# A gated MLP with quantised activations: a row of scales read back a slot later, POOL's scaling of weights moved ahead of its sums, two start loads exchanged, and the warm-up matmuls dealt out anew

## The chip, the cores and the metric

The kernel runs on one core of one Trainium2 chip. Such a core has a matrix engine (PE, TensorE) and three engines for elementwise work: DVE (VectorE), ACT (ScalarE) and POOL (GpSimd). SP (SyncE) computes nothing and issues transfers (DMAs). Each engine takes its instructions strictly in the order in which they are written for it. The metric is the time of one execution in microseconds on the device.

## The reference

There are 4 sequences of 1024 tokens with 512 features (`x`), a condition row of 128 numbers for each sequence (`cond`), and three weights: `norm_w` (512 x 128), `up_w` (4096 x 512) and `down_w` (512 x 2048).

```python
scale = cond @ norm_w.T + 1.0                    # one row of 512 scales for each sequence
ms = mean(x * x, axis=-1)
h = x * (scale[:, None, :] * rsqrt(ms + 1e-6))
u = h @ up_w.T
val, gate = split(u, 2, axis=-1)
h = val * gelu(gate)
hq = act_quant(h)        # rows scaled to +-127 by their largest value, rounded, scaled back
wq = weight_quant(down_w)                        # -1, 0 or 1 times mean(abs(down_w))
y = hq @ wq.T + x
```

## The kernel before

**Batches and slots.** The work goes batch by batch (`b`, a sequence of 1024 tokens, in two halves of 512) and in each batch slot by slot (`j`, 0 to 15, each 128 of the 2048 hidden features, with their gate and value rows of `up_w`). In the first batch the up product is made plainly: `plain_half(j, h)` makes the gate (12 matmuls, `pg`), its GELU on ACT, the value (12 matmuls, `pv`), and their product on DVE (L513). While it does so, it also prepares the weights for the later batches, which use a scheme with 7 products instead of 8 (`slot`, `product`). The lines that the change touches all lie in the first batch and its start.

**The weights of a slot** go through these steps: `w_load(j)` (SP, L244) fetches two tiles of 128x512; `w_range(j)` (DVE, L249 to L254) finds a power of two for every row and its inverse `iv`; `w_gain(j)` (DVE, L257); `w_scale(j)` multiplies the tiles by `iv` (L265, on POOL unless said otherwise); `w_turn(j)` transposes them on PE (L273) into two PSUM banks `pw`; `w_high(j)` (ACT, L286 to L289), `w_evac(j)` (ACT, L302) and `w_low(j)` (DVE, L295 to L298) take them out as a high and a low f16 part and as f32. From the f32 copy POOL makes four sums (`s_sums`, L306 to L309), ACT their high parts (`s_high`, L317), POOL their low parts (`s_low`, L321); SP writes the slot's 896 KB to DRAM (`s_spill`, L324). `s_all(j)` is s_high, s_low and s_spill. The tile that a spill has read is filled again three slots later, by `w_high`.

PSUM banks rotate: tag A has two, B one, E two, `po` three. A matmul or transpose that writes a bank waits until everything that reads the bank's earlier content is done. `pw`, `pm` and `pd` share the three banks of `po` from slot 1 on.

**The scales of cond.** `cond_scale(0)` (DVE, L160) makes batch 0's row at the start from `nw` (norm_w) and `cb` (cond's row read to all 128 partitions), both loaded on ACT's queue. `cond_largest`, `cond_over` (a PE transpose, `pm`), `cond_range`, `cond_spread` (a PE matmul, `pd`) and `cond_undo` make from it a power of two for the batch. The rows of batches 1 to 3 are made on DVE later (`cond_scale_rest`), written to DRAM four bytes at a time by `cond_rows` (SP, L214) in slot 3, and read back by `cond_load_scale(b)` (SP, L219) as a tile that all partitions hold. `cond_bring` (DVE, L223) multiplies the tile by the batch's power of two. The row of batch 1 is used first by `Tokens.scale` in slot 6.

**The start.** DVE makes an identity matrix and zeros (`warm`), from which `keep_warm(n)` issues n matmuls of 128x512 that nobody reads. The tokens of the first half are loaded in pairs (`first_load`), summed (`first_sum`, ACT, L712), scaled by the inverse root (`rsqrt_start`, ACT and DVE; `first_scale`, L729 on ACT or L731 on DVE), transposed (`first_turn`, PE, L736, four transposes for each of the tiles 0 to 3 into four banks `ptx`), and taken out by `first_high` (ACT, L740) and `first_low` (DVE, L744). The first matmuls of slot 0 (L527) follow the first_high steps one by one.

**Order.** In the start and the first batch the order is the order of the calls, written out by hand under a manual schedule; there is no planner there. Each call appends its instructions to the queues of its engines. The stretch that matters stands at lines 924 to 982, and this piece of it in slot 4 is the reading back:

```python
for j in range(3, NJ):
    if j == 4:
        sc = cond_load_scale(1)
        cond_bring(1, sc)
    first_batch(j, sc if j >= 4 else None)
```

Of the kernel before, what the change touches and what calls it, by code (L numbers as in the profile page):

```python
# [41 lines left out]
def glu_quant_kernel(  # L42
# [10 lines left out]
    PE, ACT, DVE, POOL, SP = nc.tensor, nc.scalar, nc.vector, nc.gpsimd, nc.sync  # L53
# [79 lines left out]
    def pow2_floor(t):  # L133

        ti = t.bitcast(I32)
        DVE.tensor_scalar(ti, ti, EXPONENT, None, ALU.bitwise_and)

    def bank(tag, bufs, shape=None, name=None):
        return psum.tile(shape or [P, TOK], F32, name=name or tag, tag=tag, bufs=bufs)

    def po_bank(name, shape=None):
        return bank("po", 3, shape, name)
# [10 lines left out]
    def cond_load(b0, b1):  # L153

        v = cond[b0:b1].rearrange("b c -> (b c)").partition_broadcast(P)
        ACT.dma_start(out=cb[:, b0:b1].rearrange("p b c -> p (b c)"), in_=v)
# [47 lines left out]
    def cond_undo(pd, b0, b1):  # L204
        DVE.tensor_copy(dx[:, b0:b1], pd)
        DVE.reciprocal(ux[:, b0:b1], dx[:, b0:b1])
# [9 lines left out]
    def cond_load_scale(b):  # L216

        sc = wpool.tile([P, D], F32, name=f"sc_{b}", tag="sc", bufs=1)
        SP.dma_start(out=sc, in_=rows_dram[b].partition_broadcast(P))  # L219
        return sc  # L220

    def cond_bring(b, sc):
        DVE.tensor_scalar(sc, sc, ux[:, b : b + 1], None, ALU.mult)  # L223
# [9 lines left out]
    def wn(j):  # L233
        return H[:, W_SLOT[j % 3]]

    def wf(j):

        return H[:, 11 if j == 2 else 15 + j % 2].rearrange("p t (n f) -> p (t n) f", n=2)
# [3 lines left out]
    def w_load(j, ts=(1, 0)):  # L242
        for t in ts:
            SP.dma_start(out=wn(j)[:, t], in_=up_v[j][:, t])  # L244

    def w_range(j, t0=0, t1=2):
        t = slice(t0, t1)
        am = sm.tile([P, 2], F32, name=f"wam_{j}_{t0}", tag="wam")[:, t]
        DVE.tensor_reduce(am, wn(j)[:, t], AX.X, ALU.max, apply_absolute_value=True)  # L249
        pow2_floor(am)  # L250
        DVE.tensor_scalar(sw[:, j, t], am, 2.0**-100, 1.0 / W_UP, ALU.max, ALU.mult)
        if j not in iv:
            iv[j] = sm.tile([P, 2], F32, name=f"iv_{j}", tag="iv", bufs=3)
        DVE.reciprocal(iv[j][:, t], sw[:, j, t])  # L254

    def w_gain(j):
        DVE.tensor_scalar(sg0[:, j, :], sw[:, j, :], dx[:, 0:1], None, ALU.mult)  # L257

    def w_scale(j, ts=(1, 0), eng=POOL):
        for t in ts:  # L260
            w, r = wn(j)[:, t], iv[j][:, t : t + 1]
            if eng is ACT:
                ACT.activation(w, w, AF.Copy, scale=r)
            else:
                eng.tensor_scalar(w, w, r, 1.0, ALU.mult, ALU.mult)  # L265

    def w_turn(j, banks=None, ts=(1, 0)):
        if j not in pw:
            pw[j] = banks or [po_bank(f"pw_{j}_{t}") for t in (1, 0)]
        for t in ts:  # L270
            n = 1 - t
            for k in range(NK):
                PE.transpose(  # L273
                    pw[j][n][:, k * P : (k + 1) * P], wn(j)[:, t, k * P : (k + 1) * P], ident
                )

    def a_parts(j):

        s = s_tile(j)
        return s[:, 0:2], A21[:, j % 3], s[:, 5]  # L280

    def w_high(j, ts=(1, 0)):
        gate, a21, a22 = a_parts(j)
        g, v = (p.rearrange("p (n f) -> p n f", n=2) for p in pw[j])
        if 1 in ts:
            ACT.copy(gate[:, :, 0], g)  # L286
        if 0 in ts:
            ACT.copy(a21[:, 0], v[:, 0])
            ACT.copy(a22[:, 0], v[:, 1])  # L289
# [14 lines left out]
    def s_sums(j):  # L304
        a11, a12, a21, a22 = (wf(j)[:, n] for n in range(4))
        POOL.tensor_tensor(sf[:, 0], a21, a22, ALU.add)  # L306
        POOL.tensor_tensor(sf[:, 2], a11, a21, ALU.subtract)
        POOL.tensor_tensor(sf[:, 1], sf[:, 0], a11, ALU.subtract)
        POOL.tensor_tensor(sf[:, 3], a12, sf[:, 1], ALU.subtract)  # L309
# [166 lines left out]
    def plain(j, t, h, ps):  # L476

        gate, a21, a22 = a_parts(j)
        a = [gate[:, 0], gate[:, 1]] if t else [a21, a22]
        a = [v.rearrange("p w (k f) -> p w k f", k=2) for v in a]  # L480
        terms = [(w, 1 - w, k) for k in range(NK) for w in (1, 0)]
        high = [(0, 0, k) for k in range(NK)]
        terms = high + terms if j < 2 else terms + high
        for n, (w, l, k) in enumerate(terms):
            PE.matmul(  # L485
                ps, a[k // 2][:, w, k % 2, :], XP[:, l, k, h * TOK : (h + 1) * TOK],
                start=n == 0, stop=n == len(terms) - 1,
            )
# [7 lines left out]
    def gain(g, t):  # L496
        return sg[g // NJ][:, g % NJ, t : t + 1]

    def h_half(g, h):
        return h_slots(g)[:, 0, h]  # L500
# [4 lines left out]
    def plain_half(j, h, between=nothing):  # L505
        pg = bank("A", 2, name=f"pg_{j}_{h}") if h else bank("B", 1, name=f"pg_{j}_{h}")
        plain(j, 1, h, pg)
        t1 = wpool.tile([P, TOK], F32, name=f"g_{j}_{h}", tag="t1")
        ACT.activation(t1, pg, AF.Gelu, scale=gain(j, 1))
        between()  # L510
        pv = bank("E", 2, name=f"pv_{j}_{h}")
        plain(j, 0, h, pv)
        DVE.scalar_tensor_tensor(h_half(j, h), pv, gain(j, 0), t1, ALU.mult, ALU.mult)  # L513
# [176 lines left out]
    start_t = sm.tile([P, 1], F32, name="start_t", bufs=1)  # L690
    eps = sm.tile([P, 1], F32, name="eps", bufs=1)
    DVE.memset(eps, EPS)
    ACT.dma_start(out=nw, in_=norm_w.rearrange("(k p) c -> p k c", p=P))
    cond_load(0, 1)
    ACT.activation(start_t, one, AF.Sqrt)


# [8 lines left out]
    ssq0 = sm.tile([P, 8], F32, name="ssq0", bufs=1)  # L706
    rs0 = sm.tile([P, 8], F32, name="rs0", bufs=1)
# [8 lines left out]
    def rsqrt_start(t, y):  # L716

        z = sm.tile([P, 2], F32, name="newton", tag="newton")
        ACT.activation(z, t, AF.Sqrt, scale=1.0 / D, bias=eps)
        DVE.tensor_scalar(t, t, 1.0 / D, EPS, ALU.mult, ALU.add)  # L720
        DVE.reciprocal(y, z)
        DVE.tensor_tensor(z, y, y, ALU.mult)
        DVE.scalar_tensor_tensor(z, z, -0.5, t, ALU.mult, ALU.mult)
        DVE.scalar_tensor_tensor(y, z, 1.5, y, ALU.add, ALU.mult)

    def first_scale(n, eng):
        r = rs0[:, n : n + 1]
        if eng is ACT:
            ACT.activation(X0[:, n], X0[:, n], AF.Copy, scale=r)  # L729
        else:  # L730
            eng.tensor_scalar(X0[:, n], X0[:, n], r, 1.0, ALU.mult, ALU.mult)  # L731

    def first_turn(n, pts):
        for k in range(NK):
            c = (n % NA) * P
            PE.transpose(pts[k][:, c : c + P], X0[:, n, k * P : (k + 1) * P], ident)  # L736
# [11 lines left out]
    def keep_warm(n):  # L748

        pz = bank("A", 2, name="pz")  # L750
        for i in range(n):
            PE.matmul(pz, warm[:, :P], warm, start=True, stop=True)
# [6 lines left out]
    first_load(4)  # L759
    first_load(6)  # L760
    w_load(2)
    keep_warm(12)
    first_sum(0)
    first_sum(1)
    cond_scale(0)
    mx = cond_largest(0, 1)
    pm = cond_over(mx, 0, 1, "A")
    rsqrt_start(ssq0[:, 0:2], rs0[:, 0:2])
    keep_warm(3)
    pd = cond_spread(cond_range(pm, 0, 1), 0, 1, "A")  # L770
    keep_warm(1)
    first_sum(2)
    first_scale(0, ACT)
    first_sum(3)
    w_range(0, 1, 2)
    first_scale(1, DVE)
    rsqrt_start(ssq0[:, 2:4], rs0[:, 2:4])
    w_scale(0, (1,), ACT)
    first_scale(2, ACT)
    cond_undo(pd, 0, 1)  # L780
    cond_bring_first()
    first_scale(3, DVE)
    ptx = [po_bank(f"ptx_0_{k}") for k in range(3)] + [bank("A", 2, name="ptx_0_3")]
    first_turn(0, ptx)
    keep_warm(2)
    first_turn(1, ptx)
    w_turn(0, [bank("E", 2, name=f"pw_0_{t}") for t in (1, 0)], (1,))
    first_turn(2, ptx)
    first_turn(3, ptx)
    w_high(0, (1,))  # L790
    w_range(0, 0, 1)
    w_scale(0, (0,), DVE)
    w_gain(0)
# [125 lines left out]
    def s_all(j):  # L919
        s_high(j)  # L920
        s_low(j, POOL)
        s_spill(j)
# [21 lines left out]
    cond_scale_rest()  # L944
    mx = cond_largest(1, B)
    plain_half(0, 1)
    s_all(1)
    s_sums(2)
    w_range(4)
    w_gain(4)  # L950
    w_turn(3)
    w_high(3)
    w_evac(3)
    w_low(3)
    w_scale(4)
    plain_half(1, 1)
    w_load(6)
    for n in D_LOAD[2]:
        d_load(n)
    s_all(2)  # L960
    s_sums(3)
    w_range(5)
    w_gain(5)
    w_scale(5)
    for n in D_SUM[1]:
        d_sum(n)
    w_turn(4)
# [8 lines left out]
        d_sum(n)  # L976

    for j in range(3, NJ):
        if j == 4:
            sc = cond_load_scale(1)  # L980
            cond_bring(1, sc)
        first_batch(j, sc if j >= 4 else None)

# [69 lines left out]
    for b in range(1, B):  # L1055
# [18 lines left out]
        if b + 1 < B:  # L1074
            sc = cond_load_scale(b + 1)
# [201 lines left out]
```

## Time and profile before

| | us |
|---|---|
| median of 3 runs | 762.49 (761.31 to 762.9) |
| the profiled execution, its own time | 763.18 |
| its span (first to last instruction) | 761.4 |
| PE busy | 742.7 (98%) |
| DVE busy | 554.1 (73%) |
| ACT busy | 376.7 (49%) |
| POOL busy | 199.0 (26%) |
| the largest DMA queue, share of 16 engines | 48.7% |
| mean granted TensorE clock | 0.991 |

A busy share is a mean over the whole span; TensorE is busy nearly always, so the time is its work, at the clock that it is granted, plus its idle time. The granted clock of the profile is a share of full speed: at 1.00 a matmul of 128x512 follows the one before after 0.216 us (12 in 2.59 us), at 0.50 after twice that. In the lists of waits each line names who waited and for whom, with the total in us, the number of times and the longest. In a line of a stretch stand its limits, its length, the busy time of PE, PEld (weight loads), DVE, ACT and POOL with the number of instructions, the granted clock, the mean busy share of the DMA engines and the GB/s that they moved.

### The profile page before, as it was taken

Reading aid. Unit: us, or ns where it says so; the run is one execution under the profiler, and the core shown is the slowest. Engines: PE = TensorE matmul, PEld = TensorE weight load, DVE = VectorE, ACT = ScalarE, POOL = GpSimd, SP = SyncE. Lnnn points to the kernel's source line nnn. Section 1 sums busy time; section 2 is a strip of 40 time slices with the busy share of each in tenths; the row PEclk is TensorE's granted clock in tenths of the full one; section 3 lists DMA queues with packets and bytes.
Section 4 is the critical chain, followed back from the end, with each engine's and each line's share of the span. In section 5 each row is a group of like instructions: output and inputs, shape, how many; then the busy total and the mean of one; then the engine's idle time right before and its main releaser. Section 6 shows DMA issues by size and latency. Waiting matters only on the chain.

```text
span 761.4 us, 9575 instructions
## 1 busy us (share of the span) xinstructions
PE 742.7 (98%) x3482; PEld 346.1 (45%) x3482; DVE 554.1 (73%) x800; ACT 376.7 (49%) x618; POOL 199.0 (26%) x218
## 2 busy tenths in 40 slices
PE   6999699999999999999999999999999999999998
PEld 3545345545444444444444444444444444444443
DVE  6785579988889876544779886543779887544896
ACT  4757256575334656444433666444433666332174
POOL 0397367989510020243010021153020000000100
PEclk7999999999999999999999999999999999999999
DMA  6269454888733334457832333557832333333243
GB/s 225 79 229 257 126 181 140 203 208 201 207 99 110 116 106 146 166 160 203 194 115 97 101 135 112 200 138 190 193 135 97 98 98 104 114 115 116 75 161 110
DMA packets 94360, 111.54 MB, mean 146 GB/s; under 512 B 61413, under 2 KB 62181, under 8 KB 94314
## 3 DMA queue, kind: packets, MB, share of 16 engines
q1 hardware_dynamic: 93498, 110.42, 48.7%
q10 hardware_dynamic: 816, 0.52, 0.3%
q8 instruction: 27, 0.44, 0.2%
q14 instruction: 19, 0.16, 0.1%
HBM read 74.73 MB, written 23.09 MB: 128 GB/s over the span
## 4 chain that ended last, share of the span: by engine, by line
PE 90%; DMA 4%; DVE 2%; ACT 1%; POOL 1%; issue 0%; SPq 0%; ACTq 0%; DVEq 0%; POOLq 0%
PE A L470 32%; PE E L470 16%; PE po L678 11%; PE pg L485 9%; PE pv L485 8%; PE B L470 8%; PE po_end L678 4%; DMA rows_dram<-scT 2%; PE pw L273 2%; DMA R<-in_cond_dram 1%; POOL SXY L321 1%; DMA SXY<-s_dram 1%; DMA sc<-rows_dram 1%; ACT R L740 1%; PE ptx L736 0%
## 5 line engine op out<-in xcount | busy, mean ns | idle before, releaser
L470 PEld LDWEIGHTS <-SXY 128*128 128x128 f16 x2016 | 197.1, 98 | 238.4 <-DMA SXY<-s_dram 1.0
L470 PE MATMUL A<-R,SXY 128*128 128x512 f16 x1152 | 264.8, 379 | 0.2 <-DMA SXY<-s_dram 0.2
L470 PE MATMUL E<-R,SXY 128*128 128x512 f16 x576 | 140.0, 379 | 0.0
L564 DVE SCALAR_TENSOR_TENSOR H<-A,sg,t 128x512 f32<-128x512 f32 x48 | 36.0, 750 | 81.2 <-PE A L470 81.2
L575 ACT ACTIVATE t<-t,sg 128x512 f32<-128x512 f32 x48 | 34.6, 720 | 106.5 <-DVE t L574 106.5
L678 PE MATMUL po<-wd,R 128*128 128x512 bf16 x384 | 85.3, 379 | 0.0
L678 PEld LDWEIGHTS <-R 128*128 128x128 bf16 x512 | 50.1, 98 | 60.4
L652 DVE TENSOR_TENSOR H<-H,am 128x1024 f32<-128x1024 f32 x64 | 76.2, 1216 | 0.0
L613 POOL PARTITION_ALL_REDUCE am<-R x8 | 14.6, 1820 | 221.0 <-DVE R L599 221.0
L597 DVE TENSOR_REDUCE gm<-H 128x512 f32<-128x1024 f32 x56 | 69.0, 1233 | 2.9 <-DMA wd<-tn 1.9
L470 PE MATMUL B<-R,SXY 128*128 128x512 f16 x288 | 70.0, 379 | 0.0
L574 DVE TENSOR_TENSOR t<-E,t 128x512 f32<-128x512 f32 x48 | 32.6, 679 | 49.3 <-PE E L470 49.3
L485 PE MATMUL pv<-R 128*128 128x512 f16 x246 | 61.6, 379 | 3.4 <-DVE H L513 3.4
L379 POOL TENSOR_TENSOR rs<-ssq,neghalf 128x2 f32<-128x2 f32 (+1 forms) x13 | 9.6, 738 | 206.2 <-DVE ssq L378 206.0
L485 PE MATMUL pg<-R,SXY 128*128 128x512 f16 x252 | 57.8, 379 | 0.2 <-ACT g L532 0.2
L485 PEld LDWEIGHTS <-R 128*128 128x128 f16 x366 | 36.1, 99 | 46.1 <-issue 4.8
L485 PEld LDWEIGHTS <-SXY 128*128 128x128 f16 x378 | 37.0, 98 | 42.7 <-issue 0.5
L561 ACT ACTIVATE t<-B,sg 128x512 f32<-128x512 f32 x48 | 33.0, 688 | 36.9 <-PE B L470 36.9
L660 ACT ACTIVATE H<-H 128x1024 f32<-128x1024 f32 x39 | 40.9, 1049 | 20.8 <-DVE H L652 20.8
L545 ACT COPY t<-A 128x512 f32<-128x512 f32 x48 | 28.1, 584 | 45.3 <-PE A L470 45.0
L599 DVE TENSOR_TENSOR R<-R,gm 128x512 f32<-128x512 f32 x56 | 43.2, 772 | 1.4
L556 ACT COPY v<-E 128x512 f32<-128x512 f32 x48 | 28.2, 587 | 32.4 <-PE E L470 28.9
(152 smaller groups left out, 903.1 us busy)
## 6 DMA issues: line engine op xcount, KB each, us to landing
SXY<-s_dram SPq DMA_DIRECT2D x48, 640.0 KB, 4.0
SXY<-s_dram SPq DMA_DIRECT2D x48, 256.0 KB, 4.4
s_dram<-SXY SPq DMA_DIRECT2D x11, 896.0 KB, 4.8
H<-in_L_cond_up_w_dram SPq DMA_DIRECT2D x32, 256.0 KB, 4.8
xr<-in_x_dram SPq DMA_DIRECT2D x19, 256.0 KB, 4.4
out_dram<-xr SPq DMA_DIRECT2D x19, 256.0 KB, 2.3
s_dram<-R SPq DMA_DIRECT2D x5, 896.0 KB
H<-in_x_dram SPq DMA_DIRECT2D x8, 512.0 KB, 4.8
```

The costliest lines, as they stand in the source:

```text
L470: PE.matmul(o, s[:, w, k, :], tv[:, :, c, l, k, :], start=start and n == 0, stop=stop and n == len(TERMS) - 1, skip_group_check=True,)
L485: PE.matmul(ps, a[k // 2][:, w, k % 2, :], XP[:, l, k, h * TOK : (h + 1) * TOK], start=n == 0, stop=n == len(terms) - 1,)
L556: ACT.copy(cur["v"], cur["E"])
L561: ACT.activation(cur["t1"], pb, AF.Gelu, scale=gain(g, 1))
L564: DVE.scalar_tensor_tensor(h_half(g - 1, 0), prev["A"], gain(g - 1, 0), prev["t1"], ALU.mult, ALU.mult)
L574: DVE.tensor_tensor(prev["t2"], prev["E"], prev["t2"], ALU.add)
L575: ACT.activation(prev["t2"], prev["t2"], AF.Gelu, scale=gain(g - 1, 1))
L597: DVE.tensor_reduce(gm[0], v, AX.X, ALU.max, apply_absolute_value=True)
L599: return [largest, lambda: DVE.tensor_tensor(m, m, gm[0], ALU.max)]
L652: DVE.tensor_tensor(v, v, r.to_broadcast([P, 2, TOK]), ALU.mult)
L660: ACT.activation(v, v, AF.Copy, bias=MAGIC)
L678: PE.matmul(po, q[:, h, j, a * P : (a + 1) * P], wd[:, j, :], start=j == 0, stop=j == NJ - 1,)
```

## The change

- In slot 4 nothing is read back any more. The read `cond_load_scale(1)` is issued at the head of slot 5 and the product `cond_bring(1, sc)` stands at the head of slot 6.
- `w_range(4)`, `w_gain(4)` and `w_scale(4)` come ahead of `s_all(1)` and `s_sums(2)`; before, the range and gain came behind both and the scaling behind `w_low(3)`. `w_range(5)`, `w_gain(5)` and `w_scale(5)` come ahead of `s_all(2)` and `s_sums(3)`. On POOL this puts the scaling (L265) in front of the lows (L321) and the sums (L306 to L309).
- cond's row of batch 0 is loaded in front of norm_w, on the same queue (ACT's).
- The warm-up matmuls were 12, 3, 1 and 2 (18); they are now 18, 4, 2 and 6 (30), at other places.
- In the start, `first_scale(0)` and `first_scale(1)` both run on ACT, ahead of the sums of tiles 2 and 3; the gate's weights of slot 0 are scaled on DVE instead of ACT; the scaling and turning of tiles 2 and 3 come after the gate's weights have been turned and their high part taken (`w_high(0, (1,))`).

```diff
--- before.py
+++ after.py
@@ -690,8 +690,8 @@
     start_t = sm.tile([P, 1], F32, name="start_t", bufs=1)
     eps = sm.tile([P, 1], F32, name="eps", bufs=1)
     DVE.memset(eps, EPS)
+    cond_load(0, 1)
     ACT.dma_start(out=nw, in_=norm_w.rearrange("(k p) c -> p k c", p=P))
-    cond_load(0, 1)
     ACT.activation(start_t, one, AF.Sqrt)
 
 
@@ -759,35 +759,35 @@
     first_load(4)
     first_load(6)
     w_load(2)
-    keep_warm(12)
+    keep_warm(18)
     first_sum(0)
     first_sum(1)
     cond_scale(0)
     mx = cond_largest(0, 1)
     pm = cond_over(mx, 0, 1, "A")
     rsqrt_start(ssq0[:, 0:2], rs0[:, 0:2])
-    keep_warm(3)
+    first_scale(0, ACT)
+    first_scale(1, ACT)
+    keep_warm(4)
     pd = cond_spread(cond_range(pm, 0, 1), 0, 1, "A")
-    keep_warm(1)
     first_sum(2)
-    first_scale(0, ACT)
     first_sum(3)
     w_range(0, 1, 2)
-    first_scale(1, DVE)
-    rsqrt_start(ssq0[:, 2:4], rs0[:, 2:4])
-    w_scale(0, (1,), ACT)
-    first_scale(2, ACT)
+    w_scale(0, (1,), DVE)
     cond_undo(pd, 0, 1)
     cond_bring_first()
-    first_scale(3, DVE)
+    rsqrt_start(ssq0[:, 2:4], rs0[:, 2:4])
+    keep_warm(2)
     ptx = [po_bank(f"ptx_0_{k}") for k in range(3)] + [bank("A", 2, name="ptx_0_3")]
     first_turn(0, ptx)
-    keep_warm(2)
     first_turn(1, ptx)
     w_turn(0, [bank("E", 2, name=f"pw_0_{t}") for t in (1, 0)], (1,))
+    w_high(0, (1,))
+    keep_warm(6)
+    first_scale(2, ACT)
+    first_scale(3, DVE)
     first_turn(2, ptx)
     first_turn(3, ptx)
-    w_high(0, (1,))
     w_range(0, 0, 1)
     w_scale(0, (0,), DVE)
     w_gain(0)
@@ -944,24 +944,24 @@
     cond_scale_rest()
     mx = cond_largest(1, B)
     plain_half(0, 1)
+    w_range(4)
+    w_gain(4)
+    w_scale(4)
     s_all(1)
     s_sums(2)
-    w_range(4)
-    w_gain(4)
     w_turn(3)
     w_high(3)
     w_evac(3)
     w_low(3)
-    w_scale(4)
     plain_half(1, 1)
     w_load(6)
     for n in D_LOAD[2]:
         d_load(n)
-    s_all(2)
-    s_sums(3)
     w_range(5)
     w_gain(5)
     w_scale(5)
+    s_all(2)
+    s_sums(3)
     for n in D_SUM[1]:
         d_sum(n)
     w_turn(4)
@@ -976,10 +976,11 @@
         d_sum(n)
 
     for j in range(3, NJ):
-        if j == 4:
+        if j == 5:
             sc = cond_load_scale(1)
+        if j == 6:
             cond_bring(1, sc)
-        first_batch(j, sc if j >= 4 else None)
+        first_batch(j, sc if j >= 5 else None)
```

## The prediction

> **What bounds the kernel now.** I read the page first, then TensorE's list of waits, then the chain of waits between 0 and 100 us, then tables by short stretches (for the granted clock) and the lists in order of time of ACT, DVE and POOL.
>
> The page:
> ```profile
> span 761.4 us, 9575 instructions
> PE 742.7 (98%) x3482; PEld 346.1 (45%) x3482; DVE 554.1 (73%) x800; ACT 376.7 (49%) x618; POOL 199.0 (26%) x218
> PEclk7999999999999999999999999999999999999999
> ```
> TensorE is the bound nearly everywhere. Only its idle time and the stretches at a lowered clock can be won, and the change adds no work to it but 12 warm-up matmuls. Its list of waits says where the idle time is:
> ```profile
> PE pm L185 <- DVE mx L178: 4.0, 1, 4.0
> PE pv L485 <- DVE H L513: 3.4, 1, 3.4
> PE pw L273 <- DVE SXY L295: 2.8, 1, 2.8
> PE pw L273 <- POOL H L265: 1.8, 1, 1.8
> ```
> Four single waits, 12.0 us together: one at 5.6 us, one at 50.4, two at 84.3 and 90.9. Each belongs to one part of the change. The chain of waits (start, length, what) names what stands behind the middle two:
> ```profile
> 66.17 13.29 DMA rows_dram<-scT
> 79.48 5.06 DMA sc<-rows_dram
> 84.63 0.48 DVE sc L223
> ```
> The row of scales is written to DRAM (13.29 us), read back (5.06 us), and in slot 4 DVE waits for it at L223 from 71.3 to 84.6 us. All of slot 4's DVE work stands behind that wait, so TensorE runs out of free banks twice. The clock, in stretches (last columns: granted clock, DMA share, GB/s):
> ```profile
> 6.00:8.00 2.00, 0.00 (x0) 0.00 (x0) 0.11 (x1) 0.46 (x3) 0.00 (x0) 0.94 0.74 237
> 16.00:18.00 2.00, 1.92 (x9) 1.65 (x9) 1.25 (x3) 1.27 (x3) 0.00 (x0) 0.50 0.23 60
> 18.00:20.00 2.00, 1.34 (x4) 0.43 (x4) 1.90 (x6) 1.74 (x4) 0.59 (x1) 1.00 0.45 135
> 95.00:95.50 0.50, 0.50 (x2) 0.15 (x1) 0.50 (x1) 0.50 (x3) 0.00 (x0) 0.50 0.86 332
> 96.50:97.00 0.50, 0.50 (x4) 0.22 (x3) 0.41 (x4) 0.50 (x3) 0.08 (x1) 1.00 0.05 12
> ```
> Half clock from about 7.75 to 18.0 and again from 93.1 to 96.5, each soon after one of the waits. The steps lie on a raster of 3.41 us (4.33, 7.75, ... 18.0; 93.1, 96.5).
>
> **Part 1, the row read back a slot later (slot 4 to slots 5 and 6).** Removed in slot 4: DVE's 13.3 us at L223. What is late next: w_range(7) starts at 71.3; its weights were issued at 63.9 and take 5.3 us, so they are there. It ends at 73.1; the product L513 of slot 4 then waits for its GELU (73.1 to 73.7) and ends at 74.4; the two pair_max take the 5.4 us that they take now (79.8), w_low(6) 1.3 (81.1). TensorE's first wait was for that L513 and its second for that w_low; it comes to them at 84.3 and about 87, so both go: 3.45 + 2.84 = 6.3 us. With no gap there the clock doesn't fall at 93.1. TensorE worked 2.7 us of that raster step (93.78 to 96.5) at half rate, so 1.35 us come back. Sum 7.6.
> What the moved step costs: on SP's queue the read now stands behind slot 4's load w_load(8) and spill(5), and ahead of w_load(9). It waits until the rows have landed (79.5 now); slot 5's SP work begins at about 77, so the wait shrinks from 9.6 us to some 2.5 and holds up only a load that is needed a slot later. w_load(8) is issued 10 us earlier (69.9), but lies behind the rows' slow writes and spill(4) (landed 83.0): I expect it at 83 to 84, where DVE asks at 81. That stall of 2 to 3 us is hidden: behind it stands slot 5's first L513, for which TensorE's products end only at about 85. The L223 product (0.48) comes at the head of slot 6, near 90, with the row landed at about 86: no wait.
>
> **Part 2, the scaling of weights ahead of sums on POOL.** w_turn(4) now waits for POOL from 50.4 to 52.17, since L265 stands behind s_low(1) (2.28, at 46.31) and four sums (about 2.8, at 48.54). Moved up, L265 stands behind DVE's w_range(4) instead: L249 ends at 46.77, three short DVE steps at 0.2 each (now 1.18 and 0.60 beside a busy POOL) make 47.4, and the two scalings of 0.69 end at 48.8. Gain 1.76. The price is on POOL: s_low(1) ends at 51.05 instead of 48.6, the sums at 53.9. Who waits? ACT's s_high(2) (50.7 to 53.2), behind which are two d_sum (2.3) and then w_high(4); but w_high(4) starts only at 57.2 now, held by the landing of spill(1), so ACT, free at 56.7, is not late. Spill(1) itself is issued 2.5 us later. It now lands 8.5 us after its issue, behind 2 MB of down_w, with the DMA engines full from 48 on; the packets of it start only at 53.5, so an issue at 51.1 keeps its place, with under a microsecond to spare. So the middle of ACT's and DVE's work stays where it is in time, while TensorE comes 1.76 earlier: pd needs the range that DVE has at 62.37 (or a little sooner, with POOL idler), and TensorE gets there at 62.1. I give back 0.3 (0 to 0.6; if spill(1) loses its place, up to 2.4). w_scale(5) ends near 55.7 instead of 59.2, and s_low(3) 0.4 later than now: nobody on the path. Sum 1.5.
>
> **Part 3, cond's row ahead of norm_w (ACT's queue).** DVE's first product needs both; they land at 5.3 and 7.8 now. Here the row:
> ```profile
> 5.50:5.75 0.25, 0.11 (x1) 0.00 (x0) 0.00 (x0) 0.25 (x2) 0.00 (x0) 1.00 0.22 45
> 5.75:6.00 0.25, 0.00 (x0) 0.00 (x0) 0.00 (x0) 0.25 (x2) 0.00 (x0) 1.00 0.19 35
> ```
> While cond's 64 KB are the only thing in flight, the engines move 35 to 74 GB/s (5.5 to 6.5 us), against some 400 two microseconds later. One row read 128 times is slow, and it runs alone. A rule speaks against the swap: the Trainium skill ("Trainium Kernel Development and Optimization", Key Constraints) says that transfers of all queues run on the same 16 engines and interleave, and spreading the issue saves only the sequencer's time. By it the sum is the same bytes, both land at 7.8, and the part is worth 0. By the row, the slow transfer now runs beside x's first 512 KB and norm_w follows it: not before 5.85 (its own 4.6 after an issue at 1.25), not after 8.3 (now, and half a microsecond of later issue). I take 6.8, since the idle stretch of 1 us is what can be filled.
>
> **Part 4, the start's order and the warm-up.** Let both be landed at L. DVE has the first roots at L + 2.5 (7.8 to 10.31 now). ACT then does two scalings (0.63 apart), two sums (0.70 apart) and the root (0.3), DVE's rest of it 0.75: second roots at L + 6.2. Now they are ready at 13.38, at 14.0 with L = 7.8, so this order by itself is 0.6 later. It pays on TensorE: turns 0 and 1 and the gate's weights stand ahead, and only turn 2 and one transpose wait: w_high (0.57), scale 2 (0.65), then five transposes at 0.107 or 0.215 and the hand-over. first_high is at 17.32 now. With L = 7.8 it comes at 15.9 at full clock, at 16.7 with the clock halved between 11.2 and 14.6; with L = 6.8 at 14.9. All after it follows first_high one to one: ACT's chain from it to slot 0's GELU is continuous (17.3 to 26), and TensorE waited 0.24 for that.
> The clock: the Trainium skill ("TensorE: Matmul & The Clock Gate", What's actually happening) lets it fall after an idle window of about 3.4 us. By that rule 18 matmuls ending at 6.9 leave a gap of 1.8 to 2.8 us, so full clock to the end. The trace is stricter: it fell at 7.75 after a raster step with 1.27 of 3.41 us busy (37%), and at 93.07 after 1.24 busy with no gap over 2.84, but did not at 86.25 after 1.47 (43%). Six more warm-up matmuls at 0.216 bring the first step to 70% and keep it; the second, 7.75 to 11.16, has about 1.0 busy with L = 7.8 (falls) and 1.8 with L = 6.8 (stays). So the rule gives 14.9 to 15.9, the trace 14.9 to 16.7. If the half clock lasted, keep_warm(6) would cost 2.6 us in front of turn 2 and first_high would be at 18.3. I take 15.4: gain 1.9 (between -1.0 and +2.5).
>
> **Sum** against the profiled execution: its time 763.18 is the span 761.4 and 1.8 around it. 7.6 + 1.5 + 1.9 = 11.0, so 752.2. That execution is 0.7 above the median of the runs (762.49), which I take off: **751.5**.
>
> **The rivals.**
> A, the forecast: 0.66, 749.8 to 753.0.
> B, the start brings nothing: cond's row still ends last or the clock stays halved, and keep_warm(6) stands in the way. For it: the bytes are the same, and the raster's phase is chance. Against it: the idle DMA stretch. Start 0 to -1: 753.4 to 754.4. Chance 0.16.
> C, POOL's order turns on itself: spill(1) loses its place, w_high(4) and pd move by up to 2.4, or the clogged w_load(8) makes a new wait in slot 5 or 6. For it: under 1 us to spare. 753 to 757. Chance 0.13.
> D, slower: the wait for the row moves to the head of slot 6 and is as long there. TensorE ran 12.9 us on before DVE's stop reached it (71.3 to 84.2). With DVE near 90, the row would have to land after 102 to cost anything, and after about 113 to eat the 11 us; then some 763 to 766. The rows land at 79.5 and the read takes 5: against it by 25 us. Chance 0.03.
> Same: 0.02, a mixture in which all gains are taken up elsewhere.
>
> A measurement of this kernel can tell about 0.2% (1.5 us) from no change. A, B, C lie beyond it: faster 0.95. The range takes A, B and the near part of C: 749.6 to 754.8.
>
> **What would show it.** Right: no DVE wait over 3 us for the row of scales, and no TensorE wait for L513 or L295 between 80 and 95; full clock after 93; L265 before L321 near 47 us, w_turn(4) right behind pv; cond and norm_w landed before 7.2; first_high before 16; at pd a wait under 0.6. Wrong: norm_w landing at 7.8 or later (part 3), a half clock longer than one raster step in the first 18 us (part 4), w_high(4) after 57.5 by the first_high's new time (part 2), or a wait at L223 in slot 6 that reaches TensorE (part 1).

## The result and the profile after

The changed kernel takes 754.83 us (median of 4 runs, 754.75 to 755.72), before 762.25 in the same comparison: ratio 0.9906, 95% interval 0.9889 to 0.9923. It is faster by 7.4 us, and lies just above the end of the stated range (754.8); the gain is two thirds of the 11.0 that were forecast between profiled executions. The profiled execution took 754.75, with a span of 752.9, so span against span the gain is 8.5.

The head of the page after:
```profile
span 752.9 us, 9580 instructions
PE 740.7 (98%) x3476; PEld 345.6 (46%) x3494; DVE 550.0 (73%) x800; ACT 376.9 (50%) x618; POOL 199.2 (26%) x218
PEclk9999999999999999999999999999999999999999
```
TensorE's waits after (who, for whom, total us, times, longest):
```profile
PE pm L185 <- DVE mx L178: 3.6, 1, 3.6
PE pg L527 <- ACT R L740: 1.1, 4, 0.5
PE pd L201 <- DVE dg L195: 1.0, 2, 0.6
```
Of the four waits of before, three are gone: both of slot 4 and the one for POOL. The fourth, at the start, is almost as long as it was (3.6, before 4.0), although six more warm-up matmuls now stand in front of it. At `pd` (the product that spreads batch 1's range) there is a new one: 0.65 at 62.7 us; the rest of the 1.0 is in the start.

The start of the chain of waits (start, length, what) says why:
```profile
0.72 0.43 ACTq L156
1.18 7.96 DMA R<-in_L_cond_norm_w_dram
9.24 0.31 DVE R L160 x2
...
18.31 2.43 ACT R L740 x4
```
norm_w, now the second on ACT's queue, lands at 9.13 us. Before, cond was the second and landed at 7.78. DVE's first product begins 1.35 later, and first_high (L740) comes at 18.31 instead of 17.32: the start lost 1.0 us where 1.9 were forecast to be won.

### The profile page after: what moved, and what is told of

The parts are those of the page before. It is cut to its first block, busy times and chain, and to the rows that moved or that the text cites. A ratio compares the mean times of both kernels' runs of the same rounds, so it can differ in the third digit from the quotient of the medians.

```text
span 752.9 us, 9580 instructions
## 1 busy us (share of the span) xinstructions
PE 740.7 (98%) x3476; PEld 345.6 (46%) x3494; DVE 550.0 (73%) x800; ACT 376.9 (50%) x618; POOL 199.2 (26%) x218
## 4 chain that ended last, share of the span: by engine, by line
PE 92%; DVE 2%; DMA 2%; ACT 1%; issue 1%; POOL 0%; ACTq 0%; SPq 0%; DVEq 0%; POOLq 0%
PE A L470 32%; PE E L470 16%; PE po L678 11%; PE pg L485 9%; PE pv L485 9%; PE B L470 8%; PE po_end L678 4%; PE pw L273 2%; DMA R<-in_L_cond_norm_w_dram 1%; DMA s_dram<-SXY 1%; DMA SXY<-s_dram 1%; PE ptx L736 1%; ACT R L740 0%; DVE R L744 0%; DVE H L171 0%
## 5 line engine op out<-in xcount | busy, mean ns | idle before, releaser
L678 PE MATMUL po<-wd,R 128*128 128x512 bf16 x369 | 82.4, 379 | 0.8
```

The lines of the kernel that those rows point to most:

```text
L678: PE.matmul(po, q[:, h, j, a * P : (a + 1) * P], wd[:, j, :], start=j == 0, stop=j == NJ - 1,)
```

## The experiments

The times of one comparison are set against the kernel before on the same chip (761.8 to 762.2 in the four comparisons below, on four chips; kernels of different comparisons are set side by side by their ratios or, where said, by their medians). First the parts one by one.

**The swap alone.** norm_w first in before; here:
```diff
-    ACT.dma_start(out=nw, in_=norm_w.rearrange("(k p) c -> p k c", p=P))
     cond_load(0, 1)
+    ACT.dma_start(out=nw, in_=norm_w.rearrange("(k p) c -> p k c", p=P))
```


> The kernel before with one edit: cond's row loaded in front of norm_w. Theory (the row read 128 times is slow by itself, and in front it holds up norm_w and x's first tiles on the same DMA engines): both landed near 9.1 us instead of 7.8, as in the changed kernel, first_high about 1.3 later, time 1.0 to 1.5 us above before. Rival (the landing at 9.1 comes from other things in the new start, such as warm-up or order of issue on SP): landing stays near 7.8 and the time within 0.5 us of before. The prediction on record would have it land at 6.8 and gain 1.0.

Measured: 763.45 against 761.91, ratio 1.0019 (1.0007 to 1.0031). Its chain has norm_w landing at 9.15 (7.97 after 1.18), as in the changed kernel, with the old start order and the old warm-up. So the late landing is the swap's own, and by itself it makes the kernel slower, by 1.5 us.

**The changed kernel with only the swap undone.**
```diff
+    ACT.dma_start(out=nw, in_=norm_w.rearrange("(k p) c -> p k c", p=P))
     cond_load(0, 1)
-    ACT.dma_start(out=nw, in_=norm_w.rearrange("(k p) c -> p k c", p=P))
```


> The changed kernel with that one edit undone: norm_w in front of cond's row again. Theory: landing back at 7.8, first_high at 16 to 17 instead of 18.3, time 1.3 to 2.3 us below the changed kernel, 752.5 to 753.5. Rival (the swap is not what makes the start late): the changed kernel's 754.8 within 0.5.

Measured: 752.06, ratio 0.9877 (0.9861 to 0.9892); the changed kernel has 0.9906. Its chain:
```profile
1.25 6.47 DMA R<-in_cond_dram
15.66 2.43 ACT R L740 x4
```
Landed at 7.72, first_high at 15.66, 2.65 earlier than in the changed kernel; 1.4 of it is the landing and the rest the clock, which stays at full rate here, while in the changed kernel it was halved from 12.25 to 15.66 (granted clock: third figure from the end):
```profile
12.00:13.00 1.00, 0.63 (x3) 0.50 (x2) 0.93 (x4) 1.00 (x3) 0.00 (x0) 0.62 1.05 385
```
That goes for every execution: the four with the swap undone have mean clocks of 0.999 to 1.0, the four of the changed kernel 0.995 to 0.998. The swap took 2.2 us (by the two ratios) to 2.8 us (by the medians) from this change; the kernel without it is a little below the range expected.

**Why the swap is late: one row read 128 times, or any small transfer in front?**
```diff
-        v = cond[b0:b1].rearrange("b c -> (b c)").partition_broadcast(P)
+        v = norm_w[0:P, :] if b0 == 0 else cond[b0:b1].rearrange("b c -> (b c)").partition_broadcast(P)
```


> The changed kernel, with cond's row of batch 0 (one row of 512 bytes read to 128 partitions) replaced by a plain read of as many bytes, the first 128 rows of norm_w, so that batch 0's scales are made from other numbers; every instruction and its size stay. Theory (reading one row 128 times is what holds the DMA engines): the first transfer no longer blocks; x's first tiles back at about 4.8 us, norm_w landed at 5.5 to 6.3, first_high near 14, time 3.5 to 4.5 us below the changed kernel: 750.3 to 751.3. Rival (any small transfer in front of norm_w does it, by its place in the queue): landing near 9 again and 754.8.

Measured: 751.14, ratio 0.9862 (0.9847 to 0.9877). norm_w lands at 6.45 and first_high is at 14.38. The same two stretches, 2 to 3 and 3 to 4 us, of the changed kernel and then of this one (the last two columns are the DMA share and the GB/s):
```profile
2.00:3.00 1.00, 1.00 (x4) 0.30 (x2) 0.89 (x6) 0.99 (x2) 0.00 (x0) 1.00 0.14 20
3.00:4.00 1.00, 1.00 (x4) 0.33 (x3) 0.07 (x1) 0.16 (x1) 0.00 (x0) 1.00 0.40 77
```
```profile
2.00:3.00 1.00, 1.00 (x4) 0.30 (x2) 0.89 (x6) 0.99 (x2) 0.00 (x0) 1.00 0.56 158
3.00:4.00 1.00, 1.00 (x4) 0.34 (x3) 0.07 (x1) 0.16 (x1) 0.00 (x0) 1.00 1.07 394
```
Only the source of 64 KB differs. With 128 different rows the engines move 394 GB/s in the fourth microsecond; with one row 128 times they move 77, although x's first 512 KB are issued on SP at 0.73. The repeated read doesn't just run beside the other transfers: it holds them up. The first sum over x (L712) begins at 7.62 in the changed kernel, at 4.83 before. So the place in the queue is harmless and the source is what costs. The exchange changes the tensor as well as the repetition; the kernel with the product first (below) settles that, since it reads the same row of cond, once, in the same place, and its fourth microsecond has 377 GB/s. Why a repeated row is slow stays open: the mean busy share of the engines is only 0.14 and 0.40 in those two stretches, so by the profile they are idle most of that time, and it doesn't say what they wait for.

**Part 1 alone.**
```diff
-        if j == 4:
+        if j == 5:
             sc = cond_load_scale(1)
+        if j == 6:
             cond_bring(1, sc)
-        first_batch(j, sc if j >= 4 else None)
+        first_batch(j, sc if j >= 5 else None)
```


> The kernel before with part 1 alone: row read back in slot 5, product in slot 6. Theory: both TensorE waits between 84 and 94 gone and no half clock at 93; 7.6 to 8.0 us below before, 754.2 to 754.7. Rival (part 1 is worth less by itself, because DVE's stall at w_range(8), 4.9 us in the changed kernel, reaches TensorE): 755.5 or more, with a TensorE wait for L513 or L295 after 80 us.

Measured: 754.69, ratio 0.9913 (0.9897 to 0.9929), 7.2 us below before. No TensorE wait after the one for POOL is left. One part alone makes as much as the whole change.

**Part 2 alone** (shortened):
```diff
     plain_half(0, 1)
-    s_all(1)
-    s_sums(2)
     w_range(4)
     w_gain(4)
+    w_scale(4)
+    s_all(1)
+    s_sums(2)
...
-    w_scale(4)
...
-    s_all(2)
-    s_sums(3)
     w_range(5)
     w_gain(5)
     w_scale(5)
+    s_all(2)
+    s_sums(3)
```


> The kernel before with part 2 alone: range, gain and scaling of slots 4 and 5 ahead of the lows and sums on POOL. Theory 1: w_turn(4) no longer waits (1.76 back), about 1 us is given back at pd (cond's range, 1.2 us of DVE beside a busy POOL). But the waits of slot 4 hang on the rows' write and read, which start after pd, so with them still there most of the 0.8 to 1.5 is lost again: 761.5 to 762.5. Rival: POOL's order alone gains its full 1.5: 760.7.

Measured: 761.49, ratio 1.0000 (0.9991 to 1.0008). Its waits of TensorE after 40 us, and the chain behind the first of them:
```profile
PE pv L485 <- DVE H L513: 5.1, 1, 5.1
PE pw L273 <- DVE SXY L295: 0.9, 1, 0.9
PE pd L201 <- DVE dg L195: 0.6, 1, 0.6
```
```profile
65.72 13.66 DMA rows_dram<-scT
79.40 4.89 DMA sc<-rows_dram
```
The wait for POOL is gone, and the wait for L513 has grown from 3.4 to 5.1: the row still lands at 84.3, and the matmuls behind that wait start at 87.50, before at 87.75. So nearly all that TensorE wins before slot 4 it waits there.

**Part 4 alone** (the start's calls from the first keep_warm to `w_high(0, (1,))` in the new order; norm_w first).

> The kernel before with part 4 alone: the start's new order and the warm-up dealt out anew, norm_w still first. Theory: norm_w and cond landed at 7.8, first_high at 15.7 as in the kernel with only the swap undone, against 17.3 before: 1.0 to 1.6 us below before (760.3 to 761.0). Rival (the start's gain is swallowed by the later waits of slot 4, which hang on the rows' write): within 0.4 of before.

Measured: 761.75 against 761.77, ratio 0.9999 (0.999 to 1.0008). In its profile first_high is at 15.79 and the span is 759.0, 2.4 below before's, at a granted clock of 1.0; the other runs had 0.992 to 0.998 and took 760.48 to 762.74. So the start is 1.5 earlier in the profiled execution, and the median shows nothing of it. In that execution the row is read 1.0 earlier; the other 1.4 of the 2.4 is the half clock after 93 us, which before has and this execution hasn't. The other runs' lower clocks say that they have such steps. They probably lie behind slot 4's waits, since the same start without those waits (the swap undone) kept 0.999 to 1.0; where they lie isn't on record, and what they take stays open.

**Fewer warm-up matmuls at the head** (12 for 18, norm_w first).
```diff
-    keep_warm(18)
+    keep_warm(12)
```


> The changed kernel with norm_w first and 12 instead of 18 warm-up matmuls at the head. Theory (the clock falls when less than about 40% of a raster step of 3.41 us was busy): the step that ends between 7.7 and 9.6 has too little work, one or two steps at half clock follow, first_high 0.5 to 1.5 later: 752.6 to 753.6. Rival (only a gap of over 3.4 us matters, and this one is under 4 us; or the later warm-ups are enough): full clock throughout and 752.1.

Measured: 753.75, ratio 0.9896 (0.9882 to 0.9909), against 752.06 and 0.9877 with 18. The clock in its profile:
```profile
11.00:12.00 1.00, 1.00 (x4) 0.63 (x4) 0.93 (x4) 1.00 (x3) 0.00 (x0) 0.50 1.05 385
14.00:15.00 1.00, 1.00 (x9) 0.70 (x8) 0.96 (x3) 0.38 (x1) 0.00 (x0) 1.00 0.24 90
```
Half clock for one raster step (10.2 to 13.6), after a longest gap of 3.0 us; first_high at 16.68 against 15.66. The reading of before's trace held: a step with too little work (here 0.5 of the 3.41 us before 10.2) lowers the clock, also without a gap of 3.4.

**Is there a better start, and can the wait at pd go?** Four more kernels, all with the other parts of the change.

cond's row fetched to one partition, behind norm_w, and spread by TensorE, behind 12 of the warm-up matmuls, into a bank `pc` from which DVE reads (shortened):
```diff
-    cond_load(0, 1)
+    c_row = sm.tile([1, C], F32, name="c_row", bufs=1)
+    ACT.dma_start(out=c_row, in_=cond[0:1])
...
-    keep_warm(18)
+    keep_warm(12)
+    pc = po_bank("pc", [P, C])
+    PE.matmul(pc, ones[:1, :], c_row, start=True, stop=True)
+    keep_warm(4)
...
-    cond_scale(0)
+    cond_scale(0, pc)
```


> The changed kernel with norm_w first and cond's row of batch 0 fetched once, to one partition (512 bytes), and spread to the 128 partitions by one TensorE product of ones with it, from whose bank DVE reads; the warm-up's first 18 are dealt as 12 before it and 4 after. Theory: no repeated read, norm_w landed near 5.3 bounds the start, first_high near 13.6, about 2 us below the kernel with the swap undone: 749.6 to 750.6. Rival (x's second pair of tiles, landed at 9.1 now, or the weights' tiles bound the start next): first_high at 15 or later, 751.5 to 752.1.

Measured: 751.45, ratio 0.9866 (0.9853 to 0.988), first_high at 15.03. Neither theory named what bounds it:
```profile
1.44 5.29 PE pz L753 x12
6.73 0.48 PE pc L765 x2
7.24 0.31 DVE R L160 x2
```
The warm-up itself holds the product until 6.73: its 12 matmuls take 5.29 us, twice the 2.59 of full rate, although the profile's rows show a granted clock of 1.00 there. Below such matmuls are called cold.

The product first: as the last kernel, with the row loaded ahead of norm_w, and the product behind 5 warm-up matmuls, 13 after it:

> As cond_by_pe, but cond's row (one partition, 512 bytes) is loaded ahead of norm_w, and the TensorE product that spreads it stands after 5 of the 18 warm-up matmuls instead of 12, so that a cold warm-up no longer delays it. Theory (the swap costs nothing where the row is read once; norm_w's landing near 5.4 then bounds the start): first product of DVE at 5.5 instead of 7.2, first_high near 13.4, 1.5 below cond_by_pe: 749.6 to 750.2. Rival (x's second pair or the weights' tile end last): first_high over 14.5 and 750.8 to 751.5.

Measured: 751.46, ratio 0.9862 (0.9847 to 0.9877). norm_w has landed at 6.1, later than expected, and the 13 matmuls, still cold in part (4.48 us, at full rate 2.8), hold pm until 8.94, where its input was there at 7.9; 0.5 of that reaches DVE. No gain on the kernel above; first_high at 14.51, in the rival's range, though not for the rival's reason.

pd behind the turn of slot 5's weights (in `first_batch`, with the swap undone):
```diff
         if j == 3:
-            pd = cond_spread(dg, 1, B, "po")
-            cond_undo(pd, 1, B)
             cond_rows()
...
             w_low(j + 2)
+        if j == 3:
+            pd = cond_spread(dg, 1, B, "po")
+            cond_undo(pd, 1, B)
         plain_half(j, 1)
```


> The kernel with only the swap undone, and TensorE's small product pd (with cond_undo behind it) placed after the turn of slot 5's weights instead of in front of it. Theory (part 2 gives back 0.65 us at pd, because cond's range on DVE ends late behind the landing of spill(1)): the wait for L195 after 60 us goes, 0.5 to 0.7 below 752.06: 751.4 to 751.6. Rival (the turn itself, or the bank that it needs, is as late): 752.0, with a wait for L295 or L297 in its place.

Measured: 751.41, ratio 0.9861 (0.9846 to 0.9875): by the medians of two comparisons 0.65 below 752.06, the length of the wait, which is gone.

The last two kernels' edits together (the product first, pd behind the turn):

> Both of these edits together: cond's row read once and spread by TensorE, pd after the turn. If they are independent, 2.4 below the kernel with the swap undone: 749.0 to 749.7. If the earlier start only moves TensorE into the landing of spill(1), which is paced by the down_w loads: 749.7 to 750.2.

Measured: 750.37, ratio 0.985 (0.9834 to 0.9866), above both ranges: next to the kernel with pd moved (751.41, in the same comparison) the start gave 1.0, where some 1.7 was expected.

And then with 7 instead of the 13 matmuls:

> The kernel with both edits, and 7 instead of 13 warm-up matmuls between the spreading product and pm (24 in all at the start instead of 30). In its profile the clock was cold until 6.9 us and those 13 held pm until 8.6, where DVE had its input at 7.7. Theory: pm at 7.8, everything behind it 0.5 to 0.9 earlier where the clock stays up: 749.5 to 750.0. Rival (with less warm-up the clock is raised later or falls again, and TensorE does its transposes at half rate): 750.4 or more.

Measured: 749.67, ratio 0.9843 (0.9828 to 0.9857), the lowest median of this study, 12.5 below before and (by medians of two comparisons) 5.2 below the change as it was made. Against the same kernel with 13 it shows no gain that is clear of noise: the intervals overlap, both profiled executions have a span of 748.6, and first_high comes at 14.4 here and at 14.1 there. The median is in the range expected, but pm ran at 8.43, not at 7.8: it now waits 1.8 us for DVE and no longer for the warm-up, and norm_w, landing at 6.49, bounds the start again.

## Why the prediction was wrong, point by point

**Part 3, the failed step.** The forecast held cond's 64 KB to be "the only thing in flight" from 5.5 to 6.5 us, took from that "the slow transfer now runs beside x's first 512 KB and norm_w follows it", and put the landing at 6.8. The read was not alone. In before, SP had issued x's second pair and three weight tiles by then:
```profile
1.74 0.43 SPq L701 DMA_DIRECT2D H<-in_x_dram  x1
2.20 1.66 SPq L244 DMA_DIRECT2D H<-in_L_cond_up_w_dram  x3
```
Where the row is read once (the first kernel with the spreading product, its loads on SP issued at the same times), the engines are busy in that stretch (5 to 6 us: 158 GB/s before, 375 there). Before, and then that kernel:
```profile
6.00:7.00 1.00, 0.00 (x0) 0.00 (x0) 0.00 (x0) 0.46 (x3) 0.00 (x0) 1.00 0.50 118
```
```profile
6.00:7.00 1.00, 1.00 (x4) 0.34 (x2) 0.00 (x0) 0.54 (x3) 0.00 (x0) 1.00 1.05 393
```
So the engines were slow because of the repeated read, for everybody, and what I read as free room was its cost. At the front of the queue it holds up x, the weights and norm_w; the landing went to 9.13, later than the 7.8 of before. The bounds, 5.85 to 8.3, had no end at which the transfer blocks others. The rule that speaks for a worth of 0 was closer than the reading of the row, but the measurement is below both. With a plain source the forecast landing was nearly right (6.45).

**Part 4, the order right given the landing, the clock a matter of chance.** For a landing at 7.8 and full clock first_high was forecast at 15.9; with the swap undone it came at 15.66, landed at 7.72. The stricter reading of the clock had it fall in such a start (16.7), and in the four runs it didn't. Which of the two comes probably hangs on where the raster's steps lie, and that differs from execution to execution: half clock began at 7.75 before, at 12.25 in the changed kernel and at 10.2 with 12 warm-up matmuls; without a fall the steps can't be seen. (The first step's share was also summed too low: work from 4.33 to 6.9 is 75% of 3.41 us, not 70%; nothing hangs on it.) In the changed kernel the late landing leaves 1.1 us of work in the step from 8.84 to 12.25, 33%, and the clock fell at its end. The start's term of the sum was 1.9 and measured -1.0, so this miss of 2.9 is the landing and the half clock that came with it. The -1.0 is the difference of two executions, of which before's had three steps at half clock; the same start as before has first_high at 16.4 and 17.0 in the profiles of parts 1 and 2 alone, each with two. The swap alone, 1.5 us by many runs, is the firmer figure. Rival B had about this size (0 to -1 for the start, 753.4 to 754.4), but in the main for another reason: it had cond's row land last, which was norm_w, or a clock that stays halved, which was halved for one step.

**Part 1, right, a little undersized.** From slot 3's second half to the product for the mean of the weights (`pmean`) the gain is 8.0, forecast 7.6; alone it gave 7.2. Before, and then after:
```profile
65.14 2.75 PE L485 MATMUL pg<-R,SXY 128*128 128x512 f16 x12
100.75 0.28 PE L361 MATMUL pmean<-wpart,one 128*128 128x1 f32 x2
```
```profile
64.61 2.75 PE L485 MATMUL pg<-R,SXY 128*128 128x512 f16 x12
92.25 0.28 PE L361 MATMUL pmean<-wpart,one 128*128 128x1 f32 x2
```
No stall in slot 5 or 6 reached TensorE. The forecast wait for w_load(8) was there, 4.9 instead of 2 to 3:
```profile
DVE wam L249 <- DMA H<-in_L_cond_up_w_dram: 4.9, 1, 4.9
```
and, as forecast, it was hidden: DVE then did its L513 at 88.9, and no wait of TensorE for it shows. The row's product L223 ran at 95.6, with no wait.

**Part 2, right in the sum, with two terms off.** The chain after:
```profile
48.53 1.36 POOL H L265 x2
49.89 2.26 POOL SXY L321 x2
52.17 5.56 DMA s_dram<-SXY
...
62.05 1.21 DVE dg L195
63.26 0.14 issue
63.40 0.35 PE pd L201 x2
```
The scaling, the lows and the issue of spill(1) come where they were forecast, shifted by the start's 1.0, and spill(1) kept its place (ACT's w_high(4) started at 57.81). Up to pm the gain is 2.2 (58.52 before, 57.30 after, with a start 1.0 later), since the second half of w_turn(4) had waited too; forecast 1.76. At pd 0.7 is given back, forecast 0.3. The two belong together: pd runs when DVE's range is there, at 63.26, which without the start's delay is 62.3 (forecast 62.37), and what TensorE wins beyond that it waits. L195, an operation on 3 numbers, took 1.2 us beside POOL's L321, not less than its 0.92 of before. Net 1.5, as forecast. Alone the part is worth nothing, because slot 4's wait ended at nearly the same time; it pays only once part 1 has taken that away.

**The sum** of the terms in the profiled executions is 8.0 + 1.5 - 1.0 = 8.5, and the span is 8.5 shorter. The deduction of 0.7 for a slow profiled execution was fair for before, whose medians in the later comparisons were 761.8 to 762.2.

## What to carry to other kernels

Read a slow stretch of the DMA engines twice: it may be room, or it may be a transfer that holds the others. The list of issues tells whether anything else was waiting, and an exchange of the source whether that transfer is to blame. In this kernel a load that repeats one DRAM row over all partitions belongs behind whatever is urgent, or is read once and spread on the chip. And where a later wait ends at a time of its own, take that wait away first: gains ahead of it were worth next to nothing here until then.

## What the runs showed that was not expected

- One 512-byte row read to 128 partitions, 64 KB, holds up the other transfers for two microseconds and more: 20 and 77 GB/s from 2 to 4 us with it at the head of the queue, 158 and 394 with 128 different rows, 268 and 377 with the row read once; and norm_w lands 2.7 us later than with the different rows (9.13 against 6.45).
- The clock fell after a raster step of 3.41 us that was too little busy, in before after a gap of 2.84 us and with 12 warm-up matmuls after one of 3.0 (1.7 us in the end). Warm-up matmuls can themselves be the delay while they are cold: 13 of them held pm for a microsecond, 0.5 of which reached DVE; that leaving 6 out gains time isn't shown.
- A DVE operation on 3 numbers took 1.20 us beside a POOL operation (the one on 1 number at the start, with POOL idle, 0.20), and TensorE waited 0.65 us for it until pd was moved.
